# A twelve-layer decoder on one core: another sorting network for sparsemax, and the top-1 layer's routing spread over the attention layer ahead of it

## The chip, the cores and the metric

The kernel runs on one core of one Trainium2 chip. The core has a matrix engine (TensorE: PE for its matmuls, PEld for loading the stationary operand), a vector engine (VectorE: DVE), a scalar engine (ScalarE: ACT), a general engine (GpSimd: POOL) and an engine that only issues transfers (SyncE: SP). Each works through a queue of its own, in order, and they wait for each other by semaphores; transfers (DMA) run beside them. The metric is the device time of one execution in microseconds (us); lower is better.

## What is computed

The input is x, 32 sequences of 128 tokens with 128 features, in float32, and a context of the same shape. Four blocks of attention, cross-attention and feed-forward layer follow each other; each takes the layernorm of x and adds its result to x. The change touches the last layers. Cut to them:

```python
x = x + _L2_attn_ref(_layernorm(x), ...)                    # one head
x = x + _L2_xattn_ref(ctx_1024, _layernorm(x), ctx_1024, ...)   # 16 heads, relative bias
x = x + _L2_ffn_ref(_layernorm(x), ...)                     # top-1 of 8 experts, and one shared
x = x + _L3_attn_ref(_layernorm(x), ...)                    # sparsemax over 32 patterns, 16 heads
x = x + _L3_xattn_ref(_layernorm(x), ctx_1024, ctx_1024, mask_BxSxS2_fk0, ..., 32)
x = x + _L3_ffn_ref(_layernorm(x), ...)                     # int8 by int8

def _L2_ffn_ref(x, Wr, Wu, Wg, Wd, Wu_s, Wg_s, Wd_s):       # 7 routed experts, hidden size 512
    probs = softmax(x @ Wr)
    topk_vals, topk_idx = top_k(probs, 2)
    for j in range(7):                                      # the largest alone counts
        mask = (topk_idx[..., 0] == j)[..., None]
        acc = acc + _swiglu(x, Wu[j], Wg[j], Wd[j]) * mask
    return 2.0 * topk_vals[..., :1] * acc + _swiglu(x, Wu_s, Wg_s, Wd_s)

def sparsemax(z):                                           # in _L3_attn_ref, over the 32 patterns
    z_sorted = -sort(-z)
    cum = cumsum(z_sorted)
    k = arange(1, 33)
    k_sup = sum(1.0 + k * z_sorted > cum)
    tau = (cum[k_sup - 1] - 1.0) / k_sup
    return maximum(z - tau, 0.0)
```

Sparsemax needs every row of 32 scores in descending order; 4096 tokens with 16 heads make 65,536 rows. In the kernel its threshold is the largest of the means of the first k sorted values less 1/k.

## The kernel before

x lies in SBUF as eight groups (G = 8) of four sequences (J = 4): 128 tokens on the partitions, 4 x 128 features along them. The program writes out layer after layer, and most layers are loops over the groups. Working tiles come from pools: `bbig` (four buffers of 2048 elements per partition), `gbig` (three), `gmid`, `bmid`, `small`, and `units` (four buffers for a unit of weights, 1536 elements). V, A and T are DVE, ACT and PE, P is POOL, SY is SP. All V, A and T calls go through a helper, whose line, L194, the profile shows for them; such groups are told apart by the names of their tiles.

`follow(T, A, V)` makes PE, ACT and DVE keep the order of the program in the layers 0 to 7. POOL and SP are never held to it, and from layer 8 on no engine is: a scheduler then orders instructions by when it expects them to be ready.

*Layer 7* (`attention16`, run by `run7`) takes one sequence per round, 34 rounds (`go_round`). A round transposes a sequence's probabilities, makes the scores of the next, and weights the values of the one before. The keys of a group are spread over four copies by POOL (`expand_keys`, L481). After `weighted` each round calls `next(others)`, a place for pieces of other work; before, only the six pieces of `last6` from the layer ahead are put there. Four rounds of a group end in `project`, which adds to x.

*Layer 8* works in two sides of four groups. For a side, `xs` is a table in DRAM in which each expert has a stretch of rows, padded to tiles of 256 tokens (14 tiles at most), and `ys` the table of results. Both are first filled with empty rows (L1519 to L1530). `ready` normalises a group, `gate` transposes it and makes the logits, `route` picks the expert (`first_k` compares all 8 with all 8), `place` counts the tokens per expert and works out each token's row `pos` and each tile's weights `wrow`. `send` scatters 128 tokens to `xs` (POOL, L1607; 16 per side). Per tile, `load` gathers its expert's weights into a `units` buffer (POOL, L1634), `rows` reads the tokens (SP, and a POOL copy, L1642), `up` and `down` do the matmuls, and `down` scatters the results to `ys` (POOL, L1674). `shared` is the shared expert (weights U[8]), four pieces per group. `collect` reads the results back and adds them to x. `layer8_first` does all of side 0 and the routing and sends of side 1: norm, gate, route, place and 16 sends of side 0; then three loads, all 16 shared pieces, side 1's routing; then the tile loop, in which side 1 is placed in tile 0 and sent from tile 2 on. The tiles and shared pieces of side 1 (`beside`) are handed out within layer 9.

*Layer 9* (`layer9`) runs the sparsemax layer over the groups, one step further in each of 15 slots per group: `scores(i + 1)`, `sort(i)`, `threshold(i - 1)` and `values(i - 1)`, layer 10 of group i - 2, layer 11 of group i - 3. A group's scores z are 128 x 2048 (four sequences x 16 heads x 32); `sort` reads one `bbig` buffer and writes another in each step. It is Batcher's odd-even merge sort. In the steps with d == p each of two instructions (maximum, minimum) takes 1024 elements; in the ten with d < p the first and last d elements of each block of 2p stay as they are, and are copied by ACT. `threshold` subtracts on POOL (L1829). Layers 10 and 11 take E = POOL for the groups 0 to 6 and E = DVE for group 7: L1928 multiplies by the dropout mask, L1934 divides the probabilities by their sum, L1974 and L1975 round, L1989 adds the bias, L1990 adds to x.

Of the kernel before, what the change touches and what calls it, by code (L numbers as in the profile page):

```python
# [10 lines left out]
F32 = mybir.dt.float32  # L11
# [14 lines left out]
G = 8  # L26
J = 4
# [177 lines left out]
def program(ctx, tc, cols, x, ctxt, mask, drop, dfirst, dsmall, dwide, drows, dunits, dexperts, dconst, drel, dwq, out):  # L205
# [184 lines left out]
    def normed(i):  # L390

        xn = mid.tile([128, J, D], F32, tag="xn", name="xn", bufs=2)
# [7 lines left out]
        for j in range(J):  # L400
            P.tensor_scalar(xn[:, j, :], xg[i][:, j, :], mv[:, j, 0:1], rs[:, j : j + 1], ALU.subtract, ALU.mult)
# [1109 lines left out]
    def layer8(side):  # L1511

        N = G // 2


        E = D + 1
        xs = dram.tile([TILES * TOKENS + HALF, E], F32, name=f"xs{side}", tag=f"xs{side}")
        ys = dram.tile([HALF + TILES * TOKENS, D], F32, name=f"ys{side}", tag=f"ys{side}")
        xs_rows = xs[0 : TILES * TOKENS].rearrange("(p n) e -> p n e", p=128)  # L1519
        rows = TILES * TOKENS // 128  # L1520
        number = small(rows)
        V.tensor_scalar(number[:, 0:1], K["row"], float(rows), float(HALF), ALU.mult, ALU.add)
        V.tensor_scalar(number, K["count"][:, 0:rows], number[:, 0:1], None, ALU.add)
        for a in range(0, rows, 14):
            empty = bbig((128, 14, E))
            P.memset(empty, 0.0)
            V.tensor_copy(empty[:, :, D].bitcast(I32), number[:, a : a + 14])
            SY.dma_start(out=xs_rows[:, a : a + 14], in_=empty)
            if a == 0:
                SY.dma_start(out=ys[0:HALF].rearrange("(p n) d -> p n d", p=128), in_=empty[:, 0:1, 0:D].to_broadcast([128, HALF // 128, D]))  # L1530
        xn_all = bbig((128, N, J, E))
        own = small(N * J)
        V.tensor_scalar(own, K["count"][:, 0 : N * J], 128.0, K["row"], ALU.mult, ALU.add)
        V.tensor_copy(xn_all.rearrange("p n j e -> p (n j) e")[:, :, D].bitcast(I32), own)
# [3 lines left out]
        xnTs, sums, ins, mids = {}, {}, {}, {}  # L1538

        def ready(i):  # L1540
            norm(xg[side * N + i], xn_all[:, i, :, 0:D])

        def gate(i):
            xnTs[i] = transposed(xn_all[:, i, :, 0:D], gmid(), A.copy)
            if i == 0:
                sums["l"] = acc((128, N * J, 8))
            for j in range(J):
                mm(sums["l"][:, i * J + j, :], xnTs[i][:, j * 128 : (j + 1) * 128], W["f2_Wr"])

        def route():  # L1550
            lg = sums.pop("l")
            l, m = bmid((128, N * J, 8)), small(N * J)
            V.tensor_reduce(m, lg, AX.X, ALU.max)
            V.tensor_tensor(l, lg, bc(m, 2, 8), ALU.subtract)
            A.activation(l, l, AF.Exp)
            V.tensor_reduce(m, l, AX.X, ALU.add)
            V.reciprocal(m, m)
            V.tensor_tensor(l, l, bc(m, 2, 8), ALU.mult)
            first_k(l, 8, 1, ssel, N * J)
            V.tensor_scalar(l, l, 2.0, None, ALU.mult)  # L1560
            V.tensor_tensor(l, ssel, l, ALU.mult)

            V.tensor_reduce(ww2, l[:, :, 0:7], AX.X, ALU.add)

        def place():
# [5 lines left out]
            tot, ends, keep8 = (bmid((128, 8, N * J)) for _ in range(3))  # L1571
            V.tensor_copy(tot, p[:, 1].rearrange("p (c e) -> p e c", e=8))
            P.memset(keep8, 1.0)
# [17 lines left out]
            V.tensor_tensor(spot, p[:, 0].rearrange("p (c e) -> p c e", e=8), ends.rearrange("p e c -> p c e"), ALU.add)  # L1591
# [454 lines left out]
```

## Time and profile before

| | |
|---|---|
| runs | 3003.21, 3010.7, 3012.12 us; median 3010.7 |
| the profiled execution | 2999.27 us, its span 2997.5 us |
| mean granted TensorE clock | 0.923 |
| layer 7's rounds | up to 2266 us, about 8.1 to 8.7 us each |
| layer 8, side 0: routing | 2272 to 2281; sends 2287 to 2311 |
| layer 8, side 0: tiles | first tokens transposed 2349, last down-projection 2441 |
| layer 9: starts of the eight sorts | 2478.0, 2515.8, 2568.2, 2644.9, 2709.5, 2763.7, 2819.0, 2873.7 |
| end of the last sort, end | 2927, 2997.5 |

The page of a profile gives each engine's busy time, then the span in 40 equal slices (a digit is the busy share in tenths), the transfers, the chain of waits that ended last, and the costliest groups of instructions: line, engine, operation, output and input tile with their shapes, count, then busy us, mean ns of one, and the idle time ahead of them with its releaser. Views of a stretch give the same for a part of the span, and a table of waits names what an engine waited for, how long in all, how often, and the longest. The three kinds of work in question stand in the last third of the span: layer 7 to 2266 us, layer 8 to 2478, layers 9 to 11 from there.

### The profile page before, as it was taken

How to read it: one execution, taken by the hardware profiler on the slowest of the kernel's cores; microseconds unless marked ns; L12 is line 12 of the kernel's file. 1: busy time of each engine (PE TensorE's matmuls, PEld its weight loads, DVE VectorE, ACT ScalarE, POOL GpSimd, SP SyncE). 2: the span in 40 equal slices, each digit the busy share in tenths (PEclk: the TensorE clock that was granted, in tenths of full speed). 3: DMA queues.
4: the chain of work that ended last, by engine and by line, in shares of the span. 5: the costliest groups of instructions: out<-in, count | busy, mean ns of one | idle time of the engine just before them, and what ended most of it. 6: DMA issues, size and time to landing. Idle time of an engine off the chain costs nothing. (4 is left out here: it accounts for less than half of the span.)

```text
span 2997.5 us, 55783 instructions
## 1 busy us (share of the span) xinstructions
PE 2554.4 (85%) x22535; PEld 1638.7 (55%) x22554; DVE 2093.0 (70%) x4263; ACT 1527.0 (51%) x3540; POOL 1003.2 (33%) x1033
## 2 busy tenths in 40 slices
PE   5788889999989989999998999988876989876564
PEld 3555567777744445566664444445553767544343
DVE  5777667888888756677786554468895339867873
ACT  4555445444412255666664444467772226555563
POOL 3333352232310123335451000124334365324544
PEclk8888889999999999999998999989997989997776
DMA  3000000000000000000000000000003253100000
GB/s 112 2 2 2 5 20 8 5 8 1 12 11 1 0 33 2 5 9 9 12 2 15 1 1 1 1 1 2 2 2 131 85 179 109 40 18 11 22 11 22
DMA packets 50147, 68.36 MB, mean 23 GB/s; under 512 B 3681, under 2 KB 41570, under 8 KB 49762
## 3 DMA queue, kind: packets, MB, share of 16 engines
q1 hardware_dynamic: 42608, 33.84, 3.7%
q0 software_dynamic: 6848, 27.81, 2.8%
q8 instruction: 178, 2.92, 0.4%
q10 hardware_dynamic: 434, 3.14, 0.3%
q14 instruction: 79, 0.65, 0.1%
HBM read 51.11 MB, written 13.68 MB: 22 GB/s over the span
## 5 line engine op out<-in xcount | busy, mean ns | idle before, releaser
L194 PE MATMUL ps<-cs,bbig 128*128 128x128 f32 x2208 | 328.5, 289 | 88.9 <-ACT bbig L194 34.9
L194 PEld LDWEIGHTS ps<-cs,bbig 128*128 128x128 f32 x2208 | 253.9, 146 | 192.4 <-ACT bbig L194 85.9
L194 ACT COPY bbig<-ps 128x512 f32<-128x512 f32 x418 | 228.9, 590 | 238.9 <-PE ps L194 238.9
L194 DVE TENSOR_REDUCE s<-two 128x8 f32<-128x1024 f32 (+1 forms) x192 | 234.1, 1220 | 119.6 <-PE two L194 118.3
L194 DVE TENSOR_TENSOR bbig<-bbig 128x256 f32<-128x256 f32 (+4 forms) x394 | 272.8, 742 | 18.6 <-ACT bbig L194 17.1
L194 PE MATMUL two<-xnT,u 128*128 128x512 f32 x512 | 260.8, 610 | 11.8 <-ACT bmid L194 6.3
L194 PE MATMUL acc<-bmid,u 128*128 128x512 f32 x448 | 239.4, 621 | 26.8 <-DVE bmid L194 25.2
L194 PE MATMUL two<-gbig,gmid 32*128 32x512 f32 (+1 forms) x1248 | 217.1, 570 | 2.4 <-ACT bbig L194 2.4
L194 DVE TENSOR_TENSOR bmid<-bmid,ps 128x512 f32<-128x512 f32 x192 | 130.2, 684 | 111.5 <-ACT bmid L194 91.8
L481 POOL TENSOR_SCALAR gbig<-bmid,cs 128x512 f32<-128x512 f32 x96 | 148.6, 1564 | 160.9 <-ACT bmid L194 160.9
L194 ACT ACTIVATE bbig<-two,s 128x256 f32<-128x256 f32 (+1 forms) x512 | 189.7, 419 | 20.2 <-DVE s L194 16.8
L194 ACT ACTIVATE bbig<-bbig 128x512 f32<-128x512 f32 (+1 forms) x160 | 128.1, 801 | 87.0 <-DVE bbig L194 86.6
L194 PE MATMUL ps<-cs,xn 128*128 128x128 f32 x288 | 68.9, 321 | 105.8 <-ACT xn L194 80.5
L194 ACT ACTIVATE bmid<-two 128x512 f32<-128x512 f32 x104 | 62.0, 597 | 190.5 <-PE two L194 182.1
L194 PEld LDWEIGHTS two<-xnT,u 128*128 128x128 f32 x512 | 92.2, 192 | 115.7 <-issue 55.8
L194 PEld LDWEIGHTS acc<-bmid,u 128*128 128x128 f32 x448 | 81.9, 197 | 128.9 <-DVE bmid L194 73.2
L194 ACT ACTIVATE bmid<-two,ws 128x512 f32<-128x512 f32 x128 | 85.1, 686 | 112.1 <-PE two L194 111.9
L194 ACT ACTIVATE bbig<-bbig,s 128x128 f32<-128x128 f32 x384 | 118.7, 387 | 27.1 <-DVE s L194 27.1
L1070 POOL TENSOR_TENSOR bbig<-bbig,s 128x1024 f32<-128x1024 f32 x32 | 60.6, 1892 | 214.1 <-PE two L194 152.6
L194 DVE TENSOR_TENSOR bbig<-two,s 128x1024 f32<-128x1024 f32 (+1 forms) x128 | 122.6, 958 | 8.6
L493 POOL MEMSET val<- 128x512 f32 x72 | 39.3, 549 | 257.3 <-PE acc L194 256.1
L194 PE MATMUL two<-xT,we 128*128 128x256 f32 x448 | 109.8, 400 | 8.6 <-ACT xT L194 4.2
(307 smaller groups left out, 5930.6 us busy)
## 6 DMA issues: line engine op xcount, KB each, us to landing
u<-in_units SPq DMA_DIRECT2D x10, 768.0 KB, 4.3
gmid<-in_ctx SPq DMA_DIRECT2D x16, 256.0 KB, 2.9
xs<-bbig SPq DMA_DIRECT2D x4, 903.0 KB, 5.7
xt<-xs SPq DMA_DIRECT2D x28, 129.0 KB, 2.3
x<-in_x SPq DMA_DIRECT2D x8, 256.0 KB, 7.2
gmid<-in_mask SPq DMA_DIRECT2D x8, 256.0 KB, 3.1
ys<-bbig SPq DMA_DIRECT2D x2, 1024.0 KB, 6.2
gmid<-ys SPq DMA_DIRECT2D x8, 256.0 KB, 3.9
```

The source lines that it names most:

```text
L194: d = f(*args, **kwargs)
L481: P.tensor_scalar(o[:, n, :], k, K["n4"][:, n : n + 1], None, ALU.mult)
L493: P.memset(o, 0.0)
L1070: (V if c2 else P).tensor_tensor(pr[:, four, :], pr[:, four, :], bc(nm[:, four], 2, 256), ALU.mult)
```

## The change

The sort becomes bitonic. Every one of the 15 steps now compares all 2048 elements in two instructions of 1024 (maximum, minimum). The first step of each merge (d == p) reads its second run backwards, by a step of -1 in the access pattern, so that the two runs, both descending, form one bitonic sequence. No element stays behind, and ACT copies none.

Side 0's fill, norm, gate, routing, placing, first load and sends become a generator, `ahead`, of 26 pieces, which `run7` takes up as further pieces of `others` after the six of `last6`, so in the rounds 6 to 31 of layer 7, where PE, ACT and DVE keep the order of the program. The norms of both sides move from ACT and DVE to `normed`, whose subtraction and scaling are on POOL; logits are copied to SBUF by group, and the routing is done by group, on 256 instead of 1024 compared elements at a time. The normalised tokens of side 0 lie in two `units` buffers, with an extra column for the token's number; the empty rows lie in `units` buffers of 11 rows instead of `bbig` buffers of 14, are filled by POOL, and are written to both sides' tables from the same buffer.

`layer8_rest` runs two shared pieces ahead of the first tile and one per tile after that; side 1's norms, gates and routing are spread over the tiles 0 to 4, its placing stands at tile 5, and its 16 sends at tiles 6 to 13. U[8] therefore holds a `units` buffer to the end of the loop.

In layer 10 the division by the sum goes to ACT. In layer 11 the bias is added to x on POOL right after the norm has been taken, not to the result at the end.

```diff
-    def normed(i):
+    def normed(i, xn=None):
...
-            P.tensor_scalar(xn[:, j, :], xg[i][:, j, :], mv[:, j, 0:1], rs[:, j : j + 1], ALU.subtract, ALU.mult)
+            P.tensor_scalar(xn[:, j, 0:D], xg[i][:, j, :], mv[:, j, 0:1], rs[:, j : j + 1], ALU.subtract, ALU.mult)
...
-    def layer8(side):
+    def layer8(side, tiles):
         N = G // 2
-        E = D + 1
-        xs = dram.tile([TILES * TOKENS + HALF, E], F32, name=f"xs{side}", tag=f"xs{side}")
-        ys = dram.tile([HALF + TILES * TOKENS, D], F32, name=f"ys{side}", tag=f"ys{side}")
-        xs_rows = xs[0 : TILES * TOKENS].rearrange("(p n) e -> p n e", p=128)
-        rows = TILES * TOKENS // 128
-        number = small(rows)
-        V.tensor_scalar(number[:, 0:1], K["row"], float(rows), float(HALF), ALU.mult, ALU.add)
-        V.tensor_scalar(number, K["count"][:, 0:rows], number[:, 0:1], None, ALU.add)
-        for a in range(0, rows, 14):
-            empty = bbig((128, 14, E))
-            P.memset(empty, 0.0)
-            V.tensor_copy(empty[:, :, D].bitcast(I32), number[:, a : a + 14])
-            SY.dma_start(out=xs_rows[:, a : a + 14], in_=empty)
-            if a == 0:
-                SY.dma_start(out=ys[0:HALF].rearrange("(p n) d -> p n d", p=128), in_=empty[:, 0:1, 0:D].to_broadcast([128, HALF // 128, D]))
-        xn_all = bbig((128, N, J, E))
-        own = small(N * J)
-        V.tensor_scalar(own, K["count"][:, 0 : N * J], 128.0, K["row"], ALU.mult, ALU.add)
-        V.tensor_copy(xn_all.rearrange("p n j e -> p (n j) e")[:, :, D].bitcast(I32), own)
+        per, tile_of = tiles
+        xns, xnTs, lgs, sums, ins, mids = {}, {}, {}, {}, {}, {}
+        xs, ys = both[side]
         ssel = sm.tile([128, N * J, 8], F32, tag="ssel", name="ssel", bufs=2)
         ww2, pos = (sm.tile([128, N * J], dtype, tag=name, name=name, bufs=2) for name, dtype in (("ww2", F32), ("pos", I32)))
         wrow = sm.tile([128, TILES], I32, tag="wrow", name="wrow", bufs=2)
-        xnTs, sums, ins, mids = {}, {}, {}, {}
         def ready(i):
-            norm(xg[side * N + i], xn_all[:, i, :, 0:D])
+            if i % per == 0:
+                t = tile_of(per)
+                own = small(per * J)
+                P.tensor_scalar(own, K["count"][:, 0 : per * J], 128.0, K["row"], ALU.mult, ALU.add)
+                if i:
+                    P.tensor_scalar(own, own, float(i * J * S), None, ALU.add)
+                P.tensor_copy(t.rearrange("p n j e -> p (n j) e")[:, :, D].bitcast(I32), own)
+                for k in range(per):
+                    xns[i + k] = t[:, k]
+            normed(side * N + i, xns[i])
+        def turn(i):
+            xnTs[i] = transposed(xns[i][:, :, 0:D], gmid(), A.copy)
+        def logits(i):
+            p = ps((128, J, 8))
+            for j in range(J):
+                mm(p[:, j, :], xnTs[i][:, j * 128 : (j + 1) * 128], W["f2_Wr"])
+            lgs[i] = small(J, 8)
+            A.copy(lgs[i], p)
         def gate(i):
-            xnTs[i] = transposed(xn_all[:, i, :, 0:D], gmid(), A.copy)
-            if i == 0:
-                sums["l"] = acc((128, N * J, 8))
-            for j in range(J):
-                mm(sums["l"][:, i * J + j, :], xnTs[i][:, j * 128 : (j + 1) * 128], W["f2_Wr"])
-        def route():
-            lg = sums.pop("l")
-            l, m = bmid((128, N * J, 8)), small(N * J)
-            V.tensor_reduce(m, lg, AX.X, ALU.max)
-            V.tensor_tensor(l, lg, bc(m, 2, 8), ALU.subtract)
+            l, m = lgs[i], small(J)
+            V.tensor_reduce(m, l, AX.X, ALU.max)
+            V.tensor_tensor(l, l, bc(m, 2, 8), ALU.subtract)
             A.activation(l, l, AF.Exp)
+        def pick_one(i):
+            l, m = lgs.pop(i), small(J)
+            at = slice(i * J, (i + 1) * J)
             V.tensor_reduce(m, l, AX.X, ALU.add)
             V.reciprocal(m, m)
             V.tensor_tensor(l, l, bc(m, 2, 8), ALU.mult)
-            first_k(l, 8, 1, ssel, N * J)
+            first_k(l, 8, 1, ssel[:, at])
             V.tensor_scalar(l, l, 2.0, None, ALU.mult)
-            V.tensor_tensor(l, ssel, l, ALU.mult)
-            V.tensor_reduce(ww2, l[:, :, 0:7], AX.X, ALU.add)
+            V.tensor_tensor(l, ssel[:, at], l, ALU.mult)
+            V.tensor_reduce(ww2[:, at], l[:, :, 0:7], AX.X, ALU.add)
...
+    def empty_rows():
+        rows = TILES * TOKENS // 128
+        number = small(rows)
+        P.tensor_scalar(number[:, 0:1], K["row"], float(rows), float(HALF), ALU.mult, ALU.add)
+        P.tensor_scalar(number, K["count"][:, 0:rows], number[:, 0:1], None, ALU.add)
+        for a in range(0, rows, 11):
+            n = min(11, rows - a)
+            empty = units.tile([128, n, E], F32, tag="unit", name="empty")
+            P.memset(empty, 0.0)
+            P.tensor_copy(empty[:, :, D].bitcast(I32), number[:, a : a + n])
+            for xs, ys in both:
+                SY.dma_start(out=xs[0 : TILES * TOKENS].rearrange("(p n) e -> p n e", p=128)[:, a : a + n], in_=empty)
+                if a == 0:
+                    SY.dma_start(out=ys[0:HALF].rearrange("(p n) d -> p n d", p=128), in_=empty[:, 0:1, 0:D].to_broadcast([128, HALF // 128, D]))
+            yield
     def layer8_first():
         N = G // 2
-        ready, gate, route, place, send, shared, load, rows, up, down, collect = layer8(0)
-        ready2, gate2, route2, place2, send2, shared2, load2, rows2, up2, down2, collect2 = layer8(1)
-        for i in range(N):
-            ready(i)
-            gate(i)
-        route()
-        place()
-        for i in range(N):
-            ready2(i)
-        for c in range(N * J):
-            send(c)
-        load(0)
+        ready, turn, logits, gate, pick_one, place, send, shared, load, rows, up, down, collect = layer8(
+            0, (2, lambda n: units.tile([128, n, J, E], F32, tag="unit", name="xn8")))
+        def ahead():
+            todo = {}
+            def put(n, f, *args):
+                todo.setdefault(n, []).append(lambda: f(*args))
+            fill = empty_rows()
+            for n in range(3):
+                put(n, next, fill)
+            for i in range(N):
+                for k, f in enumerate((ready, turn, logits, gate, pick_one)):
+                    put(3 + 3 * i + k, f, i)
+            put(17, place)
+            put(17, load, 0)
+            for c in range(N * J):
+                put(18 + c // 2, send, c)
+            for n in range(26):
+                for f in todo.get(n, ()):
+                    f()
+                yield
+        return ahead(), lambda: layer8_rest(shared, load, rows, up, down, collect)
+    def layer8_rest(shared, load, rows, up, down, collect):
+        N = G // 2
+        ready2, turn2, logits2, gate2, pick_one2, place2, send2, shared2, load2, rows2, up2, down2, collect2 = layer8(
+            1, (N, lambda n: bbig((128, n, J, E))))
         load(1)
         load(2)
         rows(0)
         rows(1)
-        for i in range(N):
-            for c in range(4):
-                shared(i, c)
-        for i in range(N):
-            gate2(i)
-        route2()
-        later = [lambda c=c: send2(c) for c in range(N * J)]
+        later = [lambda i=i, c=c: shared(i, c) for i in range(N) for c in range(4)]
+        later.pop(0)()
+        later.pop(0)()
         up(0)
         for t in range(TILES):
             if t + 3 < TILES:
                 load(t + 3)
             if t + 2 < TILES:
                 rows(t + 2)
+            if t < N:
+                ready2(t)
             if t + 1 < TILES:
                 up(t + 1)
+            if 0 < t <= N:
+                turn2(t - 1)
+                logits2(t - 1)
+                gate2(t - 1)
+                pick_one2(t - 1)
+            if t == N + 1:
+                place2()
             down(t)
-            if t == 0:
-                place2()
-            for _ in range(2 if t > 1 else 0):
-                if later:
-                    later.pop(0)()
+            if later:
+                later.pop(0)()
+            if t > N + 1:
+                for c in range((t - N - 2) * N * J // (TILES - N - 2), (t - N - 1) * N * J // (TILES - N - 2)):
+                    send2(c)
         for i in range(N):
...
             cur, nxt = ordered[i], bbig()
             ordered[i] = nxt
-            for half in (slice(0, 1024), slice(1024, 2048)) if d < p else (slice(0, 2048),):
-                a, b = (t[:, half].rearrange("p (n k) -> p n k", k=2 * p) for t in (cur, nxt))
-                if d < p:
-                    A.copy(b[:, :, 0:d], a[:, :, 0:d])
-                    A.copy(b[:, :, 2 * p - d :], a[:, :, 2 * p - d :])
-                    a, b = (t[:, :, d : 2 * p - d] for t in (a, b))
-                lo, hi, lo2, hi2 = (
-                    bass.AP(t.tensor, t.offset + at, [list(t.ap[0]), list(t.ap[1]), [2 * d, max(p // d - 1, 1)], [1, d]])
-                    for t in (a, b) for at in (0, d))
-                V.tensor_tensor(lo2, lo, hi, ALU.max)
-                V.tensor_tensor(hi2, lo, hi, ALU.min)
+            def side(t, at, step=1):
+                return bass.AP(t.tensor, t.offset + at, [list(t.ap[0]), [2 * d, 1024 // d], [step, d]])
+            lo, hi = side(cur, 0), side(cur, 2 * d - 1, -1) if d == p else side(cur, d)
+            V.tensor_tensor(side(nxt, 0), lo, hi, ALU.max)
+            V.tensor_tensor(side(nxt, d), lo, hi, ALU.min)
...
             for j in range(J):
-                E.tensor_scalar(pr[:, j, :], pr[:, j, :], rec[:, j : j + 1], None, ALU.mult)
+                A.mul(pr[:, j, :], pr[:, j, :], rec[:, j : j + 1])
...
         def normal():
             next(st["steps"])
+            P.tensor_tensor(xg[i], xg[i], bc(WW["qbias"], 1, J), ALU.add)
...
-            E.tensor_tensor(o, o, bc(WW["qbias"], 1, J), ALU.add)
             E.tensor_tensor(xg[i], xg[i], o, ALU.add)
...
     run5(bias7, lead7)
-    run7(last6, iter(()))
-    layer8_first()
+    ahead8, run8 = layer8_first()
+    def beside7():
+        yield from last6
+        yield from ahead8
+    run7(beside7(), iter(()))
+    run8()
     layer9()
```

## The prediction

> **What bounds the kernel now.** I read the page's head and slices first, then stretches of the layers that the diff touches, then VectorE's groups and waits there. The head of the page and its rows of 40 slices (75 us each):
>
> ```profile
> span 2997.5 us, 55783 instructions
> PE 2554.4 (85%) x22535; PEld 1638.7 (55%) x22554; DVE 2093.0 (70%) x4263; ACT 1527.0 (51%) x3540; POOL 1003.2 (33%) x1033
> ...
> PE   5788889999989989999998999988876989876564
> ...
> DVE  5777667888888756677786554468895339867873
> ```
>
> Nothing before slice 27 (about 2025 us) changes. From there the binding engine alternates: DVE in slices 27 to 29 (layer 7), PE in 31 and 32 (layer 8), DVE again from 33 (layer 9). The stretches, in columns length, PE, PEld, DVE, ACT, POOL busy (instructions), PE clock, DMA share, GB/s:
>
> ```profile
> 2100.00:2175.00 75.00, 62.48 (x813) 41.00 (x816) 62.67 (x103) 56.96 (x151) 29.96 (x38) 0.93 0.01 2
> 2175.00:2250.00 75.00, 59.18 (x830) 39.95 (x824) 69.57 (x146) 59.07 (x158) 28.14 (x37) 0.98 0.01 2
> 2250.00:2325.00 75.00, 50.73 (x328) 29.05 (x321) 39.53 (x118) 16.66 (x34) 32.00 (x37) 0.77 0.38 131
> 2325.00:2400.00 75.00, 69.62 (x338) 54.91 (x337) 27.65 (x57) 22.85 (x43) 28.41 (x36) 0.91 0.28 87
> ```
>
> Layer 7 runs DVE 84 to 93% of the time. Between 2250 and 2325 no engine is full: layer 8's opening (empty rows, routing, sends) is a serial chain. Layer 9's groups, the same columns (the first the group whose sort runs from 2478, the last two with no layer-8 work left beside them):
>
> ```profile
> 2478.00:2515.00 37.00, 35.37 (x188) 29.30 (x189) 36.30 (x60) 23.57 (x67) 19.83 (x17) 1.00 0.36 108
> 2515.00:2568.00 53.00, 48.10 (x286) 38.08 (x284) 42.50 (x65) 31.26 (x82) 27.71 (x24) 0.97 0.36 115
> 2568.00:2645.00 77.00, 68.35 (x291) 39.20 (x292) 55.61 (x105) 41.91 (x105) 23.74 (x17) 0.96 0.08 24
> ...
> 2764.00:2819.00 55.00, 34.43 (x167) 22.62 (x165) 45.84 (x97) 32.03 (x92) 25.93 (x18) 0.78 0.05 15
> 2819.00:2874.00 55.00, 34.33 (x168) 21.06 (x169) 45.97 (x97) 32.56 (x92) 26.11 (x18) 0.78 0.05 15
> ```
>
> Groups 0 to 2 are PE's (35 of 37, 48 of 53, 68 of 77); groups 4 to 7 are DVE's, 46 busy and 9 idle of 55.
>
> **1. The sort.** VectorE's groups in layer 9 (2480 to 2997 us): busy us, mean ns, idle before; then its waits from 2478 to 2927:
>
> ```profile
> L194 DVE TENSOR_TENSOR bbig<-bbig 128x1024 f32<-128x1024 f32 x64 | 82.6, 1312 | 1.7 <-ACT bbig L194 0.5
> L194 DVE TENSOR_TENSOR bbig<-bbig 128x256 f32<-128x256 f32 x128 | 66.6, 566 | 0.2
> L194 DVE TENSOR_TENSOR bbig<-bbig 128x384 f32<-128x384 f32 x96 | 55.4, 627 | 9.8 <-ACT bbig L194 9.8
> ...
> L194 DVE TENSOR_TENSOR bbig<-gbig 128x1024 f32<-128x1024 f32 x15 | 18.2, 1223 | 31.3 <-ACT gbig L194 31.3
> ```
> ```profile
> DVE bbig L194 <- ACT gbig L194: 36.9, 7, 9.9
> DVE bbig L194 <- ACT bbig L194: 17.1, 11, 4.7
> ```
>
> Before, a group's 50 max/min instructions take 33.8 us on average (30.15 where nothing disturbs; by size, end minus the later of own start and predecessor's end). After there are 30, all of 1024 elements. An undisturbed one adds 1.14 us, so 34.2, and 3.6 of disturbance as now makes 37.8: +4 per group, +32 over eight. The disturbance (about 26 us in all) falls only where a POOL tensor_tensor overlaps; none falls beside a POOL tensor_scalar.
>
> Against that: 40 ACT copies per group go (101.9 us of ACT in all), with DVE's 17.1 us of waits for them; and ACT, freed of 13 us per group, can bring z earlier, for which DVE waits 36.9. In groups 4 to 7 the idle 9 us are 4.5 for z, 3.2 for copies, 1.4 for PE (18.0, 12.6 and 5.6 of the four groups' waits). After: 46+4 busy, idle 0 to 9, so 50 to 59; with ACT freed I take an idle of 2, 52, -3 each, -12. Groups 0 to 2 gain no PE work; DVE grows from 134 to 146 of 167 us, and the surplus falls partly on the path: +4 together, from 0 (all under PE) to +12 (all on it). Group 3 (51 of 64, waits of each kind): 0, from -6 to +4. Layer 9: -8, between -26 (-20 and -6) and +32 (no wait recovered, nothing under PE).
>
> No row shows a negative step. Five of 15 steps read one operand so. Lower bound of the cost 0: the other operands keep the (p,p) steps' strides. Upper bound: the nearest odd stride, the (2,1) step with elements 16 bytes apart, 618 ns for 256 elements, 2.4 ns per element against 1.2; 10 instructions at twice 1.2 us are +12 per group, +96. I take 0: consecutive words stay consecutive. The Trainium skill ("Vector Engine (DVE) Microarchitecture Reference") says how an operand with a negative step streams was not measured.
>
> [...]
>
> **2. Side 0's first half into layer 7's rounds.** Added to DVE per group, from the rows of the same forms in layer 5: four bn_stats at 276 ns (1.1), four aggregates (0.6), three 4-wide reductions at 180 (0.5), three 32-wide operations at 224 (0.7), reciprocal 175, four of 256 at 420 (1.7), a reduction 414, two scalars 176: about 5, so 20 in four groups, and `place` 4.5 (its rows span 2282.1 to 2286.8).
>
> ```profile
> L194 DVE TENSOR_TENSOR bmid<-s 128x256 f32<-128x256 f32 x16 | 6.1, 422 | 0.2
> L194 DVE BATCH_NORM_STATS2 s<-x 128x6 f32<-128x128 f32 x76 | 17.1, 276 | 0.0
> ```
>
> Some 25 us in all; in 2025 to 2250 DVE idles 30 us of 225, three-quarters of it waiting for PE's `two`, which a later DVE also makes later. I put 15 on the path (7 if a half hides, 25 if none). PE's 16 transposes and 16 logits and ACT's 1.1 us per group fit into 13 and 16 idle us per 75; if not, they cost 5 and 4.
>
> POOL has 45 idle of 75: four norms (4.5 each), the fills (eight SP transfers, six before, into a stretch that moves 2 GB/s) fit. But in the order that the changed program is built in, 16 sends (1.26 apart, the rows of L1607) and three weight loads, the last behind all landings, stand on POOL ahead of the last group's key expansion (L481, four of 1.56). 16 x 1.26 + 4 + 2.5 + 6.2 = 33 us after `pos`; scores wait for it three rounds (26 us) on: +5 (0 to 10). Layer 7: +20 (7 to 44).
>
> **3. Layer 8.** Now layer 7's last addition ends at 2266 and the last down-projection at 2441: 175 us. PE's work in it: 14 tiles at 5.58 (2349 to 2381), 78; four shared groups at 10.8, 43; gates of both sides, some 9 of PE time each. So 139 needed, 36 lost in the opening and in the tiles of 2387 to 2413, where POOL issues sends, stores and loads together. After, the opening and one gate are gone: 78 + 43 + 9 = 130, plus 8 where the built order puts 13 sends in one bunch between two loads (13 x 1.26 = 16 us of POOL, less one tile of 8 us in hand), plus 6 for up to five more table loads (1.28 each), as gates now alternate with Silu. 144: -31. If only the opening's 2266 to 2281 goes: -15. If neither bunch nor tables cost: -45. One weight buffer fewer: a load (issue 1.3, landing 5.4) against some 11 us of PE work to the next use; hidden, and up to 14 x 2 if the cover goes, inside the -15.
>
> **4. Division and bias.** Division: POOL 4 x 1.06 becomes ACT 4 x 0.39 in seven groups (for the last DVE's 283 ns become ACT's 393, +0.4). The bias (L1989, 2.34 on POOL, 0.69 in the last group) goes into an earlier addition on POOL, which idles 29 of 55 there; uncovered it is 1.6 per group. Only the last groups' chain, 2927 to 2997, sets the end: -2 (-4 to 0).
>
> **Sum.** +20 - 31 - 8 - 2 = **-21**, on the profiled execution 2999.3 to 2978. That execution is 11 under the median of 3010.7, which I take as base: **2990**. By the terms' bounds without the negative step: -68 to +61; they do not all fall together, so its own range is 2955 to 3020.
>
> **Rivals.**
> - *VectorE is the bound all along (slower).* One mechanism: DVE's added work, 32 in layer 9 and 25 in layer 7, falls on the path, because the 54 us of waits recur elsewhere (z waits on PE's chain, not on ACT). For it: 84 to 98% DVE in layer 7 and group 0. Against: the 9 idle us in groups 4 to 7 name ACT. With 25 + 5 in layer 7, +20 in layer 9 (groups 3 to 7 pay 4 each) and layer 8 at -20: +30, 3041. It decides once layers 7 and 9 together lose more than 33 + 9 = 42.
> - *Backwards reading is slow.* +96 at most: 3086. For it: the (2,1) row; against: consecutive words.
> - *A wash.* The opening reappears in layer 7 (+31), layer 9 at 0: 3009.
> - *ACT was the brake.* Groups 4 to 7 at 50 (-20), 0 to 3 at -5, layer 7 +10, layer 8 -40, tail -2: -57, 2954.
> - *The move does not take place*, POOL being free to run fills late. The built order has `place` and sends within layer 7, so only their lateness is open; it is in the +5.
>
> **How the numbers follow.** Repeat runs differ by some 9 us, 0.3%, and less can't be told from no change. Forecast (2990) 0.39, ACT the brake 0.12: faster 0.51. A wash 0.13. VectorE the bound 0.28, backwards slow 0.08: slower 0.36. The range, 2948 to 3045, holds the forecast, the brake, the wash and the DVE case; it leaves the backwards case and tails.
>
> **What would show it.** Sort rows: 240 of 1024 at 1.2 to 1.35; about 2.4 on the five first steps would be the backwards case. Groups 4 to 7 at 52, ACT copies gone, the wait for z shorter. Layer 7's end near 2286, layer 8's last down-projection some 144 later. Wrong: layer 7's end past 2300, groups 4 to 7 at 55 or more, or layer 8 over 160.

## The result

The changed kernel took 3011.1 us against 3010.6 (medians of twelve runs each; ratio 1.0006, 95% interval 0.9989 to 1.0023). In two later sets of runs it gave 1.0028 (1.0009 to 1.0046) and 1.0019 (1.0003 to 1.0035). So it is within the 0.3% by which repeat runs differ, and if anything slower by a few microseconds; 2990, a gain of 21, was forecast. What layer 8 gains, layer 7 and the layers 9 to 11 take back.

The page of the changed kernel, profiled at 3008.7 us of span:

```profile
span 3008.7 us, 55326 instructions
## 1 busy us (share of the span) xinstructions
PE 2558.4 (85%) x22535; PEld 1637.9 (54%) x22554; DVE 2139.9 (71%) x4140; ACT 1458.3 (48%) x3272; POOL 1010.5 (34%) x1049
```

VectorE has 123 instructions fewer and 47 us more work; ACT lost 69 us. The length of each stage in us, from two traces of before and three of after (the first is the profile of the result, the others are repeat runs described below):

| stage | before | after | forecast |
|---|---|---|---|
| layer 7, first to last addition to x | 226.9, 228.8 | 267.3, 263.9, 264.7 | +20 |
| layer 8, from there to side 0's last down-projection | 177.3, 178.9 | 137.8, 136.4, 137.8 | -31 |
| from there to the first sort | 34.3, 34.8 | 35.3, 33.5, 32.7 | 0 |
| first sort to the end | 519.5, 513.4 | 527.3, 540.8, 526.5 | -10 |
| sum | 958, 956 | 968, 975, 962 | -21 |

Layer 7 grew by 37, not 20; layer 8's first side shrank by 41, not 31; layers 9 to 11 grew by some 15 instead of shrinking by 10.

**Layer 7.** The same stretch in the two kernels (columns as in the prediction: length, busy times of PE, PEld, DVE, ACT and POOL, clock, DMA share, GB/s), first before, then after:

```profile
2039.50:2266.40 226.90, 184.31 (x2504) 125.34 (x2504) 194.70 (x360) 171.08 (x453) 91.57 (x117) 0.95 0.04 14
```
```profile
2040.90:2308.20 267.30, 209.07 (x2552) 138.56 (x2550) 214.40 (x435) 176.00 (x465) 128.49 (x171) 0.87 0.05 16
```

VectorE's work grew by 20 us (25 had been summed), and the stretch by twice that. PE's busy time grew by 25 us for 48 instructions; its granted clock fell from 0.95 to 0.87. VectorE's largest wait in the stretch, for PE's scores (`two`), came as often as before and took twice as long; first before (2039 to 2266), then after (2041 to 2308):

```profile
DVE bbig L194 <- PE two L194: 19.5, 17, 3.3
```
```profile
DVE bbig L194 <- PE two L194: 37.9, 17, 7.0
```

TensorE's largest new wait in after:

```profile
PE two L194 <- POOL gbig L482: 5.6, 1, 5.6
```

That is the key expansion of the last group, standing behind the sends on POOL. With the reciprocal that ends a round's weighting as the mark, the trace gives the length of every round of layer 7 (7 to 11 us each in before, not the 8.1 to 8.7 stated ahead). Here are the second traces of both kernels:

| rounds | what is in them in after | before | after |
|---|---|---|---|
| 6 to 8 | fills | 25.2 | 25.3 |
| 9 to 22 | norms, turns, logits, routing of four groups | 124.5 | 148.9 |
| 10 alone | group 0's four transposes and their copy, nothing on VectorE | 8.7 | 12.6 |
| 22 alone | group 3's routing, VectorE only | 8.7 | 11.6 |
| 23 | `place` | 7.7 | 14.5 |
| 24 to 28 | sends | 40.1 | 47.3 (round 26: 14.3 for 7.6) |

From trace to trace the rounds 6 to 28 of before repeat to 0.1 us, but for round 7 (7.1 and 8.5). Those of after don't all: eight of the rounds 9 to 23 differ by 0.5 to 1.6 us between its three traces (round 10 took 11.2, 12.6 and 12.6), and rounds 9 to 22 together took 151.5, 148.9 and 150.5.

**Layers 9 to 11.** Groups 4 to 6 in after, and VectorE's waits in after from the first sort to the last one's end (2481 to 2938):

```profile
2717.20:2774.70 57.50, 35.61 (x190) 23.79 (x190) 52.77 (x83) 23.09 (x57) 23.73 (x14) 0.82 0.05 14
2774.70:2833.40 58.70, 35.70 (x166) 22.06 (x166) 51.78 (x78) 22.51 (x56) 23.65 (x14) 0.74 0.05 14
2833.40:2887.50 54.10, 31.00 (x166) 19.69 (x166) 51.81 (x77) 22.46 (x56) 23.88 (x14) 0.81 0.05 15
```
```profile
DVE s L194 <- POOL s L364: 17.6, 11, 9.2
DVE bbig L194 <- ACT gbig L194: 12.3, 2, 8.9
DVE bmid L194 <- ACT bmid L194: 8.5, 3, 7.2
DVE x L194 <- PE ps L194: 8.1, 9, 5.0
```

The waits for ACT's copies (17.1 us) are gone and those for z fell from 36.9 to 12.3. In their place VectorE waits for POOL's norms (3.5 before, 17.6 now, 13.6 of it in the groups 0 to 3) and for projections (2.4, now 8.1): an addition of a projection to x stands ahead of the next sort in VectorE's queue, and PE is late with it. Over the eight groups (sums of the windows) VectorE's idle time fell by 34 us, from 79.9 to 46.1, and its busy time rose by 41.5, from 369.1 to 410.6. Two kinds of its instructions in before (2480 to the end), then its groups in after (2481 to 2940):

```profile
L194 DVE TENSOR_SCALAR s<-s 128x4 f32<-128x4 f32 x37 | 12.2, 331 | 1.2 <-ACT bmid L194 0.8
...
L194 DVE SCALAR_TENSOR_TENSOR s<-s 128x4 f32<-128x4 f32 x21 | 4.1, 193 | 9.6 <-POOL s L364 9.6
```
```profile
L194 DVE TENSOR_TENSOR bbig<-bbig 128x1024 f32<-128x1024 f32 x224 | 288.0, 1312 | 1.6
L194 DVE TENSOR_TENSOR bbig<-gbig 128x1024 f32<-128x1024 f32 x16 | 22.2, 1422 | 12.3 <-ACT gbig L194 12.3
...
L194 DVE TENSOR_SCALAR s<-s 128x4 f32<-128x4 f32 x28 | 12.8, 458 | 0.0
L194 DVE SCALAR_TENSOR_TENSOR s<-s 128x4 f32<-128x4 f32 x17 | 12.4, 728 | 17.6 <-POOL s L364 17.6
```

The sort itself costs what was forecast: each instruction counted from the later of its own start and its predecessor's end, the eight sorts take 301.4 us against 270.0 and 273.4 in the two traces of before, +28 to +31 (forecast +32). An instruction that reads backwards takes 1.13 us where nothing disturbs, like the others. The other 10 us are short operations that grew. From the first sort to the end of the last one, counted in the same way, the sixteen scalar_tensor_tensor on 128x4 took 8.5 us more in all than in before (0.70 us each for 0.20), and the 27 tensor_scalar on 128x4 took 2.6 more (0.47 for 0.38). In group 5 four of them take 1.0 to 1.2 us, each beside a tensor_tensor on POOL and ending within 0.03 us of it; in before it was two. In each of the groups 3 to 6 one of them ends with L2003, the addition of layer 11's bias, which the change put there.

### The profile page after: what moved, and what is told of

It is laid out like the page before. It is cut to its first block, busy times and chain, and to the rows that moved or that the text cites. A ratio compares the mean times of both kernels' runs of the same rounds, so it can differ in the third digit from the quotient of the medians.

```text
span 3008.7 us, 55326 instructions
## 1 busy us (share of the span) xinstructions
PE 2558.4 (85%) x22535; PEld 1637.9 (54%) x22554; DVE 2139.9 (71%) x4140; ACT 1458.3 (48%) x3272; POOL 1010.5 (34%) x1049
## 4 chain that ended last, share of the span: by engine, by line
PE 52%; DVE 29%; ACT 8%; POOL 7%; issue 3%; DMA 1%; DVEq 0%; ACTq 0%; POOLq 0%; SPq 0%
PE ps L194 23%; PE two L194 15%; PE acc L194 14%; DVE bbig L194 11%; DVE s L194 10%; DVE bmid L194 4%; DVE gmid L194 3%; ACT bbig L194 3%; POOL xn L402 3%; ACT bmid L194 2%; ACT gmid L194 1%; POOL s L400 1%; POOL xs L1608 1%; POOL s L364 1%; ACT gbig L194 1%
## 5 line engine op out<-in xcount | busy, mean ns | idle before, releaser
L194 PE MATMUL ps<-cs,bbig 128*128 128x128 f32 x2192 | 335.9, 294 | 102.7 <-ACT bbig L194 35.3
L194 DVE TENSOR_TENSOR bbig<-bbig 128x1024 f32<-128x1024 f32 x232 | 297.8, 1309 | 1.6
L194 PE MATMUL acc<-bmid,u 128*128 128x512 f32 x448 | 237.0, 616 | 13.6 <-DVE bmid L194 12.3
L194 PE MATMUL two<-gbig,gmid 32*128 32x512 f32 (+1 forms) x1248 | 225.7, 600 | 8.0 <-POOL gbig L482 5.6
L194 ACT ACTIVATE bmid<-two 128x512 f32<-128x512 f32 x104 | 61.9, 597 | 170.6 <-PE two L194 170.5
L402 POOL TENSOR_SCALAR xn<-x,s 128x128 f32<-128x128 f32 x152 | 122.2, 816 | 5.3 <-PE ps L194 1.4
```

Of the source, the lines that this page charges most:

```text
L194: d = f(*args, **kwargs)
L402: P.tensor_scalar(xn[:, j, 0:D], xg[i][:, j, :], mv[:, j, 0:1], rs[:, j : j + 1], ALU.subtract, ALU.mult)
```

## The experiments

Ratios are to the kernel before, run in the same set on the same chip, with their 95% interval. The kernel before took 3008 to 3011 us in three sets of runs and 3019 to 3023 in three others, so ratios, not times, are compared across sets. I call them the 3010 sets and the 3020 sets.

**The sort alone**, in the kernel before (the new body of `sort`, all else as it was).

> The kernel before with the new sort alone. Theory (VectorE pays for whole steps): the first sort starts at 2478 us as before, from the first sort's start to the end is 8 to 14 us longer than before's 519.5, groups 4 to 6 at 56 to 59 us against 54 to 55, no sort instruction of 1024 elements slower for its negative step (1.13 us undisturbed), total +8 to +14. Rival (the recorded forecast's: ACT's copies were the brake and the surplus is in the other edits): layer 9 shorter by 0 to 10, total 0 to -10.

1.0081 (1.0053 to 1.0108), some +24 us. First sort to the end 539.2; groups 4 to 6 59.3, 57.7 and 57.8. The direction of the theory holds and the rival falls; the price is larger than the 8 to 14 expected.

**The old sort in the changed kernel**, run in two 3020 sets.

```diff
-            lo, hi = side(cur, 0), side(cur, 2 * d - 1, -1) if d == p else side(cur, d)
...
+                if d < p:
+                    A.copy(b[:, :, 0:d], a[:, :, 0:d])
...
```

> The changed kernel with the sort of before put back (copies by ACT again). Theory: layers up to the first sort as in the changed kernel (layer 7 +42, layer 8's first side -40, first sort at about 2481), layer 9 and the end about as before or 2 to 4 shorter for the division and the bias: total -1 to +3 against the kernel before in the profile, 8 to 12 under the changed kernel. Rival (the sort is neutral, the division and the bias cost what layer 9 lost): within 3 of the changed kernel.

> The changed kernel with the old sort, a second time. Theory (the stall of round 24, where TensorE fell to two or three matmuls per 1.3 us beside the sends, belongs to the chip of the first call, as do 10 us in layer 8): round 24 takes 8.9 us and round 26 14.3 as in the two traces of the changed kernel, layer 8's first side 136 to 139; total 0 to -10 against before. Rival (it belongs to this build): round 24 again at about 21.

1.0012 (0.9995 to 1.0028) and 0.9996 (0.9974 to 1.0018). First sort to the end 522.0 and 525.8, 3 to 10 us over what was foreseen (the old layers 9 to 11 themselves took 526.0 in a 3020 set, see below). Layer 7 took 272 and 271: round 24 21.1 both times, round 26 7.6. The first lines of PE's waits in round 24 and 25 (2240 to 2275) of the second one:

```profile
PE acc L194 <- issue: 8.9, 9, 1.5
PE ps L194 <- ACT bbig L194: 4.1, 3, 3.5
```

PE waits for nothing that the profile shows, and yet starts mostly two or three matmuls per 1.3 us, the distance of the sends on POOL (1.26), until the sends end. I return to this below.

**Another order in layer 7.** First the pieces freed from the kept order, then the keys put ahead of all sends but two.

```diff
+                pinned = [(e, e.kept, e.last) for e in (V, A, T)]
+                follow()
                 for f in todo.get(n, ()):
                     f()
+                for e, kept, last in pinned:
+                    e.kept, e.last = kept, last
```

> The changed kernel with the 26 pieces taken out of the kept order of PE, ACT and DVE in layer 7, so that the scheduler places them; in the built program PE's order stays and DVE's small operations stand elsewhere in the rounds. Theory (a piece costs its trip through PE and ACT ahead of a round's transposes, and VectorE's work its own length): layer 7's rounds 9 to 22 stay within 8 us of the changed kernel's +28. Rival (it is the place of DVE's work in the round that costs): most of the 28 goes, layer 7 ends 15 to 25 earlier.

1.0012 (0.9995 to 1.0029). Rounds 9 to 23 took 158.7 for 163.4 to 166.1 in the three traces of after; so VectorE's operations elsewhere in the round save 5 to 7, not 15 to 25. Round 24 stalled (22.7).

```diff
+            if side == 0:
+                tc.add_manual_dep(d.ins, spread[0].ins.name, info, reason="the keys first")
```

> The changed kernel with all but two of side 0's sends put behind the last group's key expansion on GpSimd. Theory (the 6.6 us of round 26 are the sends in front of the keys): round 26 back to within 1.5 us of before's 7.6, layer 7's end 5 to 7 earlier, the first tile of layer 8 0 to 5 earlier than now as its rows then wait for later sends; total -3 to -6. Rival (round 26's wait has another cause, the load behind all landings or the lower PE clock): round 26 stays at 12 to 14.

1.0063 (1.0036 to 1.0090): slower by 19. Round 26 came down to 8.8, but round 25 took 27.6: now the cleared value tile of the next sequence (a POOL memset) stood behind the sends, and PE was slow beside them as in round 24 above. Moving one waiter ahead of the bunch exposed the next.

**The changed kernel and the kernel before again.**

> The kernel before, unchanged, for a second trace beside the others. Theory: layer 7's rounds within 0.5 us of the first trace each; first sort to the end 518 to 522; what the first trace has less than the median of 3010.7 lies ahead of layer 7. Rival (layers 8 and 9 themselves vary by 10 us from run to run): first sort to the end, or layer 7's end to the last down-projection, off by over 5 us.

> The changed kernel, unchanged, for a second trace. In three relatives of it, whose layer 7 is built alike, TensorE fell to two or three matmuls per 1.3 us while side 0's sends were issued (rounds 24 or 25 took 21, 23 and 28 us against 8.9 in the first trace of the changed kernel). Theory (the stall belongs to the sends beside layer 7 and varies with where in the program it falls): this trace shows it again or not, but layer 7's rounds 9 to 23 repeat to 0.5 us each. Rival (it belongs to the chip of that call): with the same program the stall appears on one chip and not on another.

> The changed kernel a third time. Theory (the stall beside the sends goes with the chip): if the kernel before takes about 3020 on this chip, round 24 takes about 21 us and round 26 7.6; if it takes about 3010, 8.9 and 14.3. Rival (it goes with the build): 8.9 and 14.3 on any chip.

Before 1.0007 (0.9986 to 1.0028), after 1.0028 and 1.0019; the stages are in the table above. Layers 7 and 8 repeat to 2 to 4 us, though not every round does. Layers 9 to 11 vary by 6 in before, more than the theory allowed, and by 14 in after: there the groups 5 and 6 take either about 54.3 or about 58 us, the longer ones with 4 to 5 us of waiting for PE's projection, and group 4 takes 57.5 to 61.9. Round 24 took 9.0, round 26 14.3, in all three traces. All were in 3010 sets, so they can't tell whether the stall goes with the set or with the build.

**The division back on POOL.**

```diff
-                A.mul(pr[:, j, :], pr[:, j, :], rec[:, j : j + 1])
+                E.tensor_scalar(pr[:, j, :], pr[:, j, :], rec[:, j : j + 1], None, ALU.mult)
```

> The changed kernel with the division in layer 10 back on GpSimd (VectorE for the last group). Theory (with the sort now keeping VectorE at its two-input operations all along, GpSimd's work beside it costs): first sort to the end 4 to 9 us longer than the changed kernel's 527. Rival (a tensor_scalar on GpSimd does not touch VectorE, as in the trace of before): within 2.

1.0045 (1.0026 to 1.0065), beside 1.0028 for the changed kernel in that set; first sort to the end 539.3, as with the sort alone. The changed kernel's own traces run from 526.5 to 540.8, so the division's worth, some 5 us, lies within the scatter: not settled.

**Pieces done twice.** `turn_again` repeats a group's transposes and copy, `rank_again` its `first_k`.

```diff
+            for i, k in ((0, 5), (1, 8)):
+                put(k, turn_again, i)
+            for i, k in ((2, 14), (3, 16)):
+                put(k, rank_again, i)
```

> The changed kernel with four pieces done twice in layer 7's rounds, the results of the second time unused: the transposes and their copy by ACT of group 0 in round 11 and of group 1 in round 14, and the comparison of the eight experts (six VectorE instructions, some 2.5 us) of group 2 in round 20 and of group 3 in round 22. Theory (every piece costs its trip): rounds 11 and 14 longer by 1.3 to 2.5 each, rounds 20 and 22 by 2 to 2.8 each. Rival (the forecast: PE and ACT have room, VectorE hides a part): rounds 11 and 14 longer by 0 to 0.4, rounds 20 and 22 by 1 to 1.7.

1.0011 (0.9989 to 1.0033). Against the second trace of after, round 11 is unchanged (9.3) and round 14 longer by 1.2; rounds 13 and 16 are shorter by 1.1 and 1.6. In these two the granted clock was 0.99 and 0.95 instead of 0.74 and 0.65, so what the extra transposes cost and what the clock gave can't be told apart. Round 22 is longer by 2.3, for 2.1 us more of VectorE's work (it took 11.6 in all three traces of after). Round 20 took 11.1, as it did in two of the three without doubling. Rounds 9 to 22 together took 151.1 us, within the 148.9 to 151.5 of after, with some 4 us more of VectorE's work. So neither the theory of a price per trip of PE and ACT nor its rival is confirmed.

**Is it the clock?** In round 10 of the second trace of after PE runs at little more than half speed: eight matmuls of `two` and eight transposes, and the same in before's second trace:

```profile
2091.04 2.09 PE L194 MATMUL two<-gbig,gmid 32*128 32x512 f32 x8
2093.06 1.97 PE L194 MATMUL ps<-cs,bbig 128*128 128x128 f32 x8
```
```profile
2091.32 1.14 PE L194 MATMUL two<-gbig,gmid 32*128 32x512 f32 x8
2093.24 1.14 PE L194 MATMUL ps<-cs,bbig 128*128 128x128 f32 x8 [0.79 <-ACT bbig L194]
```

The Trainium skill ("TensorE: Matmul & The Clock Gate", Part 1) says that the array falls to half its clock after an idle window. The rows agree in kind. To see whether that costs time, PE was given useless work:

```diff
+                if warm[0] and r == 0:
+                    for _ in range(12):
+                        turn_over(t[:, 0, :], ident)
```

> The changed kernel with twelve useless transposes of the identity ahead of each round's first real ones, in rounds 6 to 31 of layer 7 (written where the real ones follow; nothing reads them). Theory (the gaps that the pieces open in TensorE's stream lower its granted clock, and the matmuls after them take twice as long): granted clock in layer 7 from 0.87 to 0.93 or more, rounds 10, 13, 14, 16 and 19 together 8 us or more shorter than the changed kernel's 60.6, in spite of some 1.7 us more work in each. Rival (the clock only goes along; the pieces' order costs): the same five rounds no shorter, or longer by 2 to 8.

> The kernel before with the same useless transposes in rounds 6 to 31. Theory (its clock is at 0.95 and has little to gain): layer 7 between 4 us shorter and 10 longer, by what the transposes cost where TensorE is on the path. Rival for h1's reading (the transposes help for another reason, by shifting the order of buffers): layer 7 shorter by 8 or more here too.

Layer 7's stretch (2044 to 2312) with it:

```profile
2044.00:2312.00 268.00, 223.52 (x2848) 165.12 (x2847) 215.73 (x439) 178.14 (x470) 130.75 (x172) 0.94 0.05 16
```

1.0029 (1.0010 to 1.0047); in the kernel before 1.0017 (0.9999 to 1.0035), with layer 7 at 230.3. The clock is back at 0.94, and the stretch as long as ever: rounds 9 to 22 took 149.0 us (148.9 to 151.5 without), the five rounds named 58.8 (57.4 to 60.5). The clearest part is rounds 9 to 14, which ran at a granted clock of 1.00 with the useless transposes in both kernels: 63.3 in after and 53.2 in before, 10.1 apart; without them it was 64.8 to 65.5 and 54.7, 10.1 to 10.8 apart. So the lower clock is not what costs there. In single rounds it may: round 16 took 12.1 us at a clock of 0.65, 11.6 at 0.78 and at 0.85 (the three traces of after), and 10.5 at 0.95 with the doubled pieces.

**Pieces earlier in the round**, ahead of the second half of the exponentials (`next(others)` ahead of `e(1)` in `go_round`), and the same with paced sends and layers 9 to 11 as before.

> The changed kernel with the pieces taken up earlier in each round of layer 7, ahead of the second half of the exponentials instead of behind the weighted values. Theory (a piece's cost beyond VectorE's own length is the PSUM buffer that ACT frees only behind the exponentials): rounds 10, 13, 16 and 19, with the transposes in them, 1 to 2 us shorter each (48.7 together now), rounds 22 and 23, with VectorE's work alone, within 0.5. Rival (a round pays for any PE-ACT trip, wherever it stands): the four rounds within 1.5 of 48.7 together, or longer.

> Paced sends, layers 9 to 11 as before, and the pieces earlier in the rounds. Theory: 4 to 8 us under the version without this, so about 0.994 to 0.996 of the kernel before. Rival: 0.9965 or more.

1.0024 (1.0004 to 1.0044) and 0.9962 (0.9945 to 0.9979), the second between its theory and its rival. Rounds 10, 13, 16 and 19 fell to 31.7 together, below before's 33.8, but with the pieces ahead of the mark their cost shows one round earlier, so this confirms nothing. Rounds 8 to 23 together took 167.1 for 171.4 to 174.4. So the place in the round is worth 4 to 7 of the 31 to 34 us by which these rounds exceed before's 140.2.

**Paced sends.** Each send is ordered behind the reciprocal of its own round, so that on POOL's queue keys and value tiles stand between them; with the new sort, with the old one, with layers 9 to 11 wholly as before, and that with the useless transposes.

```diff
-            V.reciprocal(rec, yd[:, 1])
+            lately[0] = V.reciprocal(rec, yd[:, 1])
...
+            if side == 0:
+                tc.add_manual_dep(d.ins, lately[0].ins.name, info, reason="two a round")
```

> The changed kernel with side 0's 16 sends paced: each is ordered behind the reciprocal of its round of layer 7, so that on GpSimd's queue the keys and the cleared value tiles of the last group stand between them. Theory (round 26's 6.6 us are the keys standing behind a bunch of sends; the keys first alone only moved the wait to the value tiles): rounds 24 to 28 within 1 us of before's each, layer 7 6 to 7 shorter than now (257 to 259), first tile not over 3 later; total 4 to 8 under the changed kernel. Rival (the sends cost by their number, wherever they stand): layer 7 stays at 263 to 268.

> Paced sends and the old sort, division and bias as in the changed kernel. Theory (the new sort costs 10 to 16 us in layer 9): first sort to the end 516 to 522, total 6 to 14 under the kernel before. Rival (the sort is neutral): no faster than the paced kernel with the new sort.

> Paced sends, and layers 9 to 11 wholly as before (old sort, division on GpSimd, bias at the end). Theory (division and bias are worth 0 to 3 with the old sort, whose ACT copies left ACT little room): within 4 of the last one, total 6 to 14 under the kernel before. Rival (the division and the bias are the gain of layer 9): 4 or more over the last one.

> Paced sends, layers 9 to 11 as before, and the useless transposes. Theory: layer 7 8 to 18 under the 268 of the version without them, total 8 to 18 under that version, so 16 to 28 under the kernel before (0.991 to 0.995). Rival: no faster than 0.9968.

| version | ratio to before | layer 7 | first sort to end |
|---|---|---|---|
| paced, new sort | 0.9993 (0.9975 to 1.0012) | 267.5 | 539.5 |
| paced, old sort | 0.9976 (0.9958 to 0.9994) | 269.7 | 530.1 |
| paced, layers 9 to 11 as before | 0.9968 (0.9948 to 0.9989) | 268.0 | 526.0 |
| the same with useless transposes | 0.9965 (0.9949 to 0.9982) | 258.0 | 519.5 |

The first three ran in one 3020 set with the second run of the old sort, whose round 24 took 21.1; with paced sends it took 8.9 in each, and round 26 7.6. But in those three round 27 took 13.7 for 7.4, with PE slow again beside the last sends, so that layer 7 did not fall to the 257 to 259 of the theory. In the fourth, run in a 3010 set, rounds 24 to 28 took 41.2, as in before (40.1); its ratio is no better for the useless transposes. Old sort and old layers 9 to 11 come out better, by 5 and 2 us, but the intervals overlap both times.

## Why the prediction was wrong

Two of the three signs of being wrong came: layer 7 ended past 2300 (at 2308), and the groups 4 to 6 took 54 to 62 us, most of them over 55.

**Layer 8's opening: right, undersized.** -31 forecast, -41 measured. The first tile's tokens are transposed as layer 7 ends. In the first trace PE was busy 126.8 us of these 137.9 (130 had been summed) and idle 11.1 (14 had been added for a bunch of sends and for table loads). The five more table loads came, 8 for 3; PE's largest wait, 4.1 us, is for a gathered unit of weights.

**"I put 15 on the path" (layer 7): the failing step.** Of VectorE's 25 us, 10 were taken to hide, because it idled 30 of 225 us waiting for PE, and the pieces of PE and ACT were put at nothing, because they "fit into 13 and 16 idle us per 75". Here is what rounds 9 to 23 show, as growth over before in the three traces of after:

| rounds | VectorE's busy time | length |
|---|---|---|
| 13, 16, 19, 22: the larger part of a group's routing | +13.8 | +13.3 to 13.9 |
| 9, 12, 15, 18: a group's norms | +5.2 | +1.9 to 3.2 |
| 23: `place` | +4.8 | +6.8 |
| 10, 11, 14, 17, 20, 21: transposes, logits, little on VectorE | +0.2 to 1.1 | +8.4 to 10.5 |

The routing lies on the path at its full length, `place` at more, and of the norms' 5 us 2 to 3 hide: together 22 to 23 us, not 15. The rounds with hardly any new work for VectorE cost another 8 to 10, where the sum had nothing (its bounds had 9). Over all of layer 7, VectorE's waits for `two` doubled. My reading is that in a kept order an engine's idle time is its wait for the other two within the same cycle, so that work put into the cycle lengthens it; this is argued, not shown, and the doubled pieces, some 4 us of VectorE's work without a visible price over the rounds together, speak against it as a general rule. What of round 10's growth is order and what is the wait for a PSUM buffer is open: pieces elsewhere in the round save 4 to 7 us in all, and the clock is not the main part.

**The keys behind the sends: right.** 5 (0 to 10) forecast, 6.7 measured in round 26, with the wait named above.

**"With ACT freed I take an idle of 2" (layer 9): the other failing step.** The sort's price was right (+28 to +31 for +32). The idle time of groups 4 to 6 is 2.3 to 9.3 us over three traces, not 2; ACT's copies and z had stood in front of the next wait, PE's projection. And VectorE's short operations grew by 11, for which the sum had nothing: more of them stand beside a tensor_tensor on POOL and end with it. That nothing is disturbed beside a POOL tensor_scalar was not quite so in before either: beside the rounding (L1974 and L1975) two sort instructions of 256 elements took 0.75 us for 0.34. The recorded rival that VectorE is the bound in both layers, with the waits recurring elsewhere, describes layers 7 and 9 in kind; layer 8 paid for it, so that the time is that of the wash, whose chance was put at 0.13, though not by its mechanism.

**Backwards reading and the division.** Of the 96 us that bounded the price of reading backwards none came, as taken. The tail after the last sort, for which -2 was forecast, is 70.0 to 70.4 us against 70.5.

## What to carry to other kernels

Idle time of an engine in a loop of engines that wait for each other in a fixed order is not room until a run has shown it: here 24 us of VectorE's work, with pieces for PE and ACT, lengthened fifteen rounds by 31 to 34. What is moved into such a loop must save more at its old place. When a wait is taken from the engine that bounds a stage, look for the wait that stands next in its queue, and for its short operations beside another engine's long ones. Issue scatters a few at a time between the other work of their engine: the bunch here delayed whatever stood behind it.

The new sort by itself cost some 24 us. The move by itself was about even (layer 8 -41 for layer 7 +37; with the old sort 1.0012 and 0.9996) and paid with paced sends: with the old layers 9 to 11 they are 0.3 to 0.4% under the kernel before.

## What was not expected of the hardware

Beside a bunch of 16 indirect sends, PE fell to mostly two or three matmuls per 1.3 us, and round 24 or 25 took 20 to 28 us instead of 9, in five traces of four builds, all in 3020 sets; six traces of other builds in 3010 sets show none of it. In the former the first side of layer 8 took 144 to 147 us, in the latter 136 to 138 (versions with the bunch or paced alike, one at 141). The first side of layer 8 as it was before took 190 in the kernel with the new sort alone, in a 3020 set, and 177 to 183 in the traces of 3010 sets. No build was profiled in both kinds of set, so for the stall it is open whether the set or the build decides; that the kernel before itself takes some 10 us longer in the 3020 sets is shown. The chip alone may not decide it: the record has the same chip number for one set of each kind. Pacing the sends removed the stall of round 24 where it was.
